# Four-layer image network on one core, scan layer: y kept in the order of the scan in two buffers, its copy-out in two halves, empty turns around the DMAs of the normalizations

## The chip, the core and the metric

The kernel runs on one core of a Trainium2 chip. The metric is the device time of one execution in microseconds. The kernel before takes 12470.36 us (median of 3 runs, 12468.33 to 12488.72).

The engines go by short names: PE multiplies matrices, ACT applies functions and copies, DVE and POOL work element by element, SP issues the DMAs. Each executes its own list of instructions in the order in which the program emits them; what one needs of another it waits for. A wait therefore holds up everything behind it on its engine.

## The reference, cut to what matters

Four layers follow one another on a tensor of 8 images x 64 channels x 64 x 64. Only the first, the scan layer, is touched. For each image it normalizes over the channels, projects to 128 channels (and a gate z), convolves 3x3 to get u, and then runs a recurrence over the 4096 pixels in four directions k: 0 along rows, 1 along columns, 2 and 3 the same two backwards.

```python
def step(h, inp):
    u_t, dt_t, B_t, C_t = inp
    h = h * jnp.exp(dt_t[..., None] * A) + dt_t[..., None] * B_t[:, :, None, :] * u_t[..., None]
    return (h, jnp.einsum('bkcn,bkn->bkc', h, C_t))
...
y = out_y[:, 0] + inv[:, 0] + wh + invwh
...
y = _ln(y, outnorm_g, outnorm_b, LN_EPS) * jax.nn.silu(z)
return jnp.einsum('bhwd,cd->bhwc', y, outproj_w) + outproj_b
```

h has 16 states n for each of the 128 channels. y is the sum over the 16 states and over the four directions, put back into the order of rows; it is normalized over the channels (the output norm), multiplied by the gate and projected back.

## The kernel before

**Tiling.** The 128 channels lie on the partitions. An image has 16 steps s: four directions, each in four chunks of 1024 pixels. The directions follow one another in the order 0, 2, 1, 3 (the last image: 1, 3, 0, 2), so steps 0 to 7 go along rows and 8 to 15 along columns. A step has 16 units, one for each state n, and the program is written as one long list of *turns*, one turn for a unit (the loop at L919). The whole list is laid down by hand (manual_schedule), so the order on each engine is the order of emission.

**A unit (L757).** ACT makes a = exp(dt x A) (L719). z = B x dt x u comes in one of two ways. For the 12 states outside BY_POOL, PE spreads B over the partitions into PSUM (L737) and DVE multiplies it (L764). For states 0, 3, 6 and 8, POOL multiplies a broadcast B loaded by DMA (L727) and ACT copies it to PSUM (L734). DVE scans (L768), POOL multiplies by the broadcast C (ct, L773), and PE adds the product into the PSUM tile yps (L810). The broadcast tiles of C come by a DMA of 512 KB each on SP's queue (L715), into five buffers; a load has to wait until PE has read the buffer's former content.

**The sum of a step.** There is a single yps tile. Products trail the units by three turns. In turn 3 of a step, the last step's sum has just been completed in turn 2, so `empty` (L779) has ACT copy it into y (L783), and `begin_sum` (L790) starts the next sum by a matmul that adds what y holds already: the identity (or, for the last sums, the centring matrix lno_cen) times y, or in the first direction skipd times u (L801). Turn 7 does two sum_ups to catch up. At two steps of an image (3 to 4 and 11 to 12), where a direction turns round on the same chunk, yps is simply kept: no copy and no begin. So an image has 14 copies and 14 begins. y lies in the order of rows, in one of two buffers that alternate by image. In the column steps (k odd), `ordered` (L588) makes a view with a step of 64 elements, and both the copy (write) and the begin (read) go through it.

**The background queue (L166 to L231).** All other work of the layer is cut into small items (a make, mostly one matmul on PE, and a use one turn later, on ACT or DVE): the projections of the next step (`lower`, `step_size`), the whole preparation of the next image (loads of x, input norm `norm_x`, projections, gates, convolution in five pieces a block), and the output norm of the image before (`norm_y`, `after`). One item is taken per turn (`bg.before`, L926 and L931). In the turns named `idle` (3, 6, 7, 8; L898) only an item without a make may be taken. `none` is an item that does nothing: an empty turn. Items of the next step go ahead of the others; pieces of the convolution alternate with the queue.

**A normalization** computes variances on PE, and ACT puts each as a row and SP sends it to DRAM (`put`, L335). Then a chain (L358) follows: `fetch` reads all variances back over 128 partitions (DMA, L345), `root` (ACT, L348), `invert` (DVE, L351, then a DMA to DRAM, L352), `back` (DMA, L356). Then `apply` has PE spread the result (L393, L445), DVE multiply by it (L398, L450) and ACT add gain and bias; for the output norm POOL multiplies by the gate (L566) and PE projects (L572, L573). The output norm of image b-1 is queued in step 0 of image b; its blocks of x and of z are loaded by two DMAs per block (L559, L561), the first three blocks at once, just before `back` (L459). The last image's own output norm goes two blocks at a time in steps 13 to 15, with two items taken per turn, and the last two blocks follow after the last unit.

Of the kernel before, what the change touches and what calls it, by code (L numbers as in the profile page):

```python
# [165 lines left out]
class Background:  # L166
# [7 lines left out]
    def __init__(self):  # L174
        self.queue, self.last, self.late = deque(), None, []
        self.groups, self.open, self.done = deque(), deque(), {}
        self.first = self.credit = 0
        self.item = False

# [42 lines left out]
    def finish(self, b, count):  # L222

        while self.done.get(b, NBK) < count:
            self.credit = 1
            self.before(slots=NBK)
            self.after()

# [6 lines left out]
def scan_layer(cm, x_in, w, xh):  # L235

    tc, nc = cm.tc, cm.nc
    with ExitStack() as ctx:
# [90 lines left out]
        def inverse_root(nb):  # L329
# [27 lines left out]

            chain = [none, (None, fetch), none, (None, root), (None, invert), none, (None, back), none]  # L358
            return put, chain, sm

        def norm_x(xn, pairs, project_in):

# [47 lines left out]
            for i in pairs:  # L410
                out += [project_in(2 * i), project_in(2 * i + 1)]
                if i + 2 in pairs:
                    out.insert(-1, apply(i + 2))
            return out

        def norm_y(y, blocks, load, multiply, project_out):
# [40 lines left out]
            out = [(None, lambda _: [square(j) for j in blocks[:2]]), none]  # L457
            out += [variance(j) for j in blocks] + chain
            out.insert(-2, (None, lambda _: [load(j) for j in blocks[:3]]))  # L459
            out += [apply(j) for j in blocks[:2]]  # L460
# [3 lines left out]
            for j in blocks:  # L464
                if j + 2 in blocks:
                    out.append(apply(j + 2))
                    if j + 2 == blocks[-1]:
                        out.append(end)
                out.append(project_out(j))
            return out  # L470
# [4 lines left out]
        def before(b):  # L475
# [72 lines left out]
            for pairs in FIRST if b == 0 else (range(NBK // 2),):  # L548
                items.append(norm_x(xn, pairs, project_in))
            return u, zd, items, [gate(j) for j in range(NBK)], [convolve(j) for j in range(NBK)]  # L550
# [226 lines left out]
        full = []  # L777

        def empty():  # L779

            if full:
                ctl = full.pop()
                nc.scalar.copy(  # L783
                    ordered(ctl["y"], ctl["k"], ctl["c"]),
                    ctl["ps"].rearrange("p (a b) -> p a b", b=S),
                )

        kept = []

        def begin_sum():  # L790


            ctl = pending[0][0]
            if kept:
                ctl["ps"] = kept.pop()
                return
            ctl["ps"] = psy.tile([DI, CH], F32, name="yps", tag="yps")
            wt, src = (skipd, ctl["u"]) if ctl["new_y"] else (ctl["mat"], ctl["y"])
            so, half = ordered(src, ctl["k"], ctl["c"]), BK // S
            for i in range(CH // BK):  # L800
                nc.tensor.matmul(  # L801
                    ctl["ps"][:, bass.ts(i, BK)].rearrange("p (a b) -> p a b", b=S),
                    wt, so[:, i * half : (i + 1) * half, :], start=True, stop=False,
                )
# [26 lines left out]
        def prepare(b, s):  # L831

            if b not in images:
                return None
            u, zd, y = images[b]
# [8 lines left out]
            ctl = dict(  # L844
                k=k, c=c, u=u, y=y, dt=dt, bc=low["bc"][k // 2], ut=ut, dus=e, soft=soft, new=new, state=None,
                first=(i == 0), new_y=(s < NCH), turns=(s % (2 * NCH) == NCH - 1),
# [9 lines left out]
        def start(b):  # L856
            u, zd, items, gates, convs = before(b)
            y = io.tile([DI, L], F32, name="y", tag="y")
            images[b] = (u, zd, y)
            bg.add(items[0] + items[1])  # L860
# [11 lines left out]
        with tc.manual_schedule():  # L872
# [15 lines left out]
            for b in range(NB):  # L888
                for s in range(4 * NCH):
# [29 lines left out]
                    for n in range(N):  # L919
# [30 lines left out]
                        if s == 0 and n == LAG + 2 and b > 0:  # L950
                            bg.add(after(b - 1, images[b - 1][2], images.pop(b - 1)[1]))
                        if late and n == LAG + 2:
                            c = 4 * NCH - s
                            bg.add(after(b, images[b][2], images[b][1], range(2 * c, 2 * c + 2)))
                        if s == (1 if b else NCH) and n == 0 and b + 1 < NB:
# [9 lines left out]
            empty()  # L965
            bg.add(after(NB - 1, images[NB - 1][2], images[NB - 1][1], range(2)))
            bg.drain()
# [1148 lines left out]
```

## Time and profile before

One execution was profiled. Its parts (windows of the trace; the scan layer's units run from the first to the last L768):

| what | us |
|---|---|
| time of the profiled execution | 12474.25 |
| its span | 12472.4 |
| before the first unit | 93.48 |
| units of the scan layer, 8 images x 16 steps | 7074.05 |
| of it: POOL busy | 6680.89 |
| of it: DVE busy | 6564.59 |
| of it: PE busy | 6497.71 |
| of it: ACT busy | 4898.81 |
| all behind the last unit (rest of the layer, the other three layers) | 5304.9 |
| image 0 / image 1 / image 3 / image 7 | 939.39 / 869.32 / 870.31 / 913.96 |

The profile's page gives busy time by engine, then the span in slices, the DMA queues, the chain of work that ended last, and groups of instructions by line. In a group's row, the count stands behind the x, then the busy time in us and the mean of one in ns, and behind the bar the idle time of the engine just before these instructions with what ended it. A window's row gives start and end, length, then the busy time of PE, weight loads, DVE, ACT and POOL (with counts), the clock granted to PE (1.00 is full), the busy share of the DMA engines and GB/s. One float32 matmul of 512 columns stands in the trace as two PE records.

### The profile page before, as it was taken

The page shows a single profiled execution, that of the slowest core. Times are in us where ns is not written, and L with a number is a line of the kernel's source. Part 1 is how long each engine was busy: PE and PEld are TensorE (multiplying, and loading weights), DVE is VectorE, ACT ScalarE, POOL GpSimd, SP SyncE. Part 2 cuts the span into 40 slices and gives each one's busy share as a digit, 9 for nine tenths or more (in the row PEclk, how much of TensorE's full clock was granted, in tenths as well). Part 3 has the DMA queues.
Part 4 walks back from the last instruction along what each step waited for, and adds up shares of the span by engine and source line. Part 5 has one row for each costly group of instructions (what it writes and reads, how often), then busy time and mean ns, then how long its engine had stood idle before and what let it go on. Part 6 is the DMA issues. An engine that isn't in the chain of part 4 may idle for free. (4 is left out here: it accounts for less than half of the span.)

```text
span 12472.4 us, 119759 instructions
## 1 busy us (share of the span) xinstructions
PE 11350.5 (91%) x38827; PEld 4100.1 (33%) x38827; DVE 10374.0 (83%) x7334; ACT 7820.0 (63%) x10296; POOL 7404.9 (59%) x3510
## 2 busy tenths in 40 slices
PE   7899998999999999999998889999987778999999
PEld 2233332332333323323322232332334463333333
DVE  4999999999999999999989857768687785676767
ACT  4776766766766767767666545546456584555554
POOL 4999999999999999999999800000005490000000
PEclk8999999999999999999989889999998789999999
DMA  3666656656666666666566510000011100000000
GB/s 110 208 210 211 210 200 221 211 202 214 210 203 212 207 212 213 202 218 205 198 206 204 179 34 18 12 25 6 18 38 40 41 24 23 17 6 17 6 11 6
DMA packets 541331, 1562.17 MB, mean 125 GB/s; under 512 B 127360, under 2 KB 144400, under 8 KB 538128
## 3 DMA queue, kind: packets, MB, share of 16 engines
q1 hardware_dynamic: 540688, 1554.36, 37.8%
q8 instruction: 310, 5.08, 0.2%
q14 instruction: 333, 2.73, 0.1%
HBM read 1456.41 MB, written 88.87 MB: 124 GB/s over the span
## 5 line engine op out<-in xcount | busy, mean ns | idle before, releaser
L773 POOL TENSOR_TENSOR ct<-ct,h 128x1024 f32<-128x1024 f32 x2048 | 4796.5, 2363 | 391.5 <-DMA ct<-bc 183.9
L768 DVE TENSOR_TENSOR_SCAN h<-a,state,z 128x1024 f32<-128x1024 f32 x1536 | 3572.4, 2342 | 96.0 <-ACT z L734 43.0
L1117 DVE TENSOR_TENSOR sum<-sum,ex 128x1024 f32<-128x1024 f32 x1920 | 2347.5, 1223 | 617.9 <-ACT ex L1110 483.0
L1110 ACT ACTIVATE ex<-sc 128x1024 f32<-128x1024 f32 x2048 | 1968.0, 1024 | 1359.7 <-PE sc L1105 1359.3
L810 PE MATMUL yps<-ct,ident 128*128 128x512 f32 x5632 | 2810.5, 629 | 6.9 <-POOL ct L773 6.8
L719 ACT ACTIVATE a<-dt,amat 128x1024 f32<-128x1024 f32 x2048 | 2345.0, 1146 | 718.1 <-DVE h L768 711.7
L764 DVE TENSOR_TENSOR z<-z,e 128x1024 f32<-128x1024 f32 x1536 | 1865.9, 1215 | 310.9 <-PE z L737 196.0
L1124 PE MATMUL av<-ex,v 128*64 128x512 f32 x8192 | 1950.0, 604 | 0.0
L1105 PE MATMUL sc<-q,k 16*128 16x512 f32 (+1 forms) x8192 | 1562.2, 623 | 4.2 <-ACT q L1098 3.1
L810 PEld LDWEIGHTS yps<-ct,ident 128*128 128x128 f32 x5632 | 1009.0, 194 | 1390.9 <-issue 1253.2
L737 PE MATMUL z<-bs,pick 48*128 48x512 bf16 x3072 | 957.0, 393 | 447.0 <-DVE h L768 398.5
L810 PE MATMUL yps<-ct,lno_cen 128*128 128x512 f32 x2560 | 1313.1, 646 | 0.5 <-POOL ct L773 0.5
L768 DVE TENSOR_TENSOR_SCAN h<-a,z 128x1024 f32<-128x1024 f32 x512 | 1163.1, 2283 | 80.8 <-ACT z L734 51.2
L727 POOL TENSOR_TENSOR bt<-bt,e 128x1024 f32<-128x1024 f32 x512 | 1210.8, 2365 | 4.5 <-DMA bt<-bc 4.5
L1431 POOL TENSOR_TENSOR gt<-gt,pad 128x1024 f32<-128x1024 f32 x16 | 34.9, 2184 | 1571.1 <-ACT gt L1430 1492.5
L1124 PEld LDWEIGHTS av<-ex,v 128*64 128x64 f32 x8192 | 512.2, 136 | 1332.8 <-issue 1278.9
L734 ACT COPY z<-bt 128x1024 f32<-128x1024 f32 x512 | 519.7, 1015 | 589.0 <-POOL bt L727 316.4
L1105 PEld LDWEIGHTS sc<-q,k 16*128 16x128 f32 (+1 forms) x8192 | 528.4, 184 | 1016.1 <-issue 977.2
L737 PEld LDWEIGHTS <-pick 48*128 48x128 bf16 x3072 | 177.7, 95 | 1709.6 <-DVE h L768 888.0
L810 PEld LDWEIGHTS yps<-ct,lno_cen 128*128 128x128 f32 x2560 | 468.6, 198 | 637.3 <-issue 560.7
L530 PE MATMUL vps<-pad,convd 128*128 128x512 f32 x1152 | 545.9, 597 | 0.0
L1804 DVE RECIPROCAL r<-e 128x512 f32<-128x512 f32 x128 | 420.6, 3322 | 0.0
(416 smaller groups left out, 10539.4 us busy)
## 6 DMA issues: line engine op xcount, KB each, us to landing
ct<-bc SPq DMA_DIRECT2D x2048, 512.0 KB
bt<-bc SPq DMA_DIRECT2D x512, 512.0 KB
x<-x SPq DMA_DIRECT2D x12, 2048.0 KB
bc<-e SPq DMA_DIRECT2D x128, 128.0 KB
zd<-z SPq DMA_DIRECT2D x64, 256.0 KB
z<-zd SPq DMA_DIRECT2D x64, 256.0 KB
x<-x SPq DMA_DIRECT2D x32, 512.0 KB
part<-x SPq DMA_DIRECT2D x128, 128.0 KB
```

The source lines that it names most:

```text
L530: nc.tensor.matmul(held[0].rearrange("p (r c) -> p r c", c=S), convd[:, t, :], pad[:, j * rows + dy : (j + 1) * rows + dy, dx : dx + S], s ...
L719: ctl["exp", n] = nc.scalar.activation(ctl["a", n], ctl["dt"], AF.Exp, scale=amat[:, ctl["k"], n : n + 1])
L727: nc.gpsimd.tensor_tensor(bt, bt, ctl["dus"], ALU.mult)
L737: nc.tensor.matmul(z[:, bass.ts(i, BK)], pick[:, n : n + 1].to_broadcast([3 * N, DI]), ctl["bs"][:, bass.ts(i, BK)], start=True, stop=True,)
L764: first = nc.vector.tensor_tensor(z, z, ctl["dus"], ALU.mult)
L768: nc.vector.tensor_tensor_scan(h[:, flip], a[:, flip], z[:, flip], 0.0 if state is None else state[:, n : n + 1], ALU.mult, ALU.add,)
L773: freed[at] = nc.gpsimd.tensor_tensor(ct, ct, h, ALU.mult)
L810: nc.tensor.matmul(ctl["ps"][:, bass.ts(i, BK)], ctl["mat"], ct[:, bass.ts(i, BK)], start=False, stop=(n == N - 1 and not ctl["turns"]),)
L1105: nc.tensor.matmul(sc[:, e, :], k[r : r + d, bass.ts(j, 128)], qs[i][r : r + d, :], start=True, stop=True,)
L1110: nc.scalar.activation(ex, sc, AF.Exp)
L1117: nc.vector.tensor_tensor(sums[i], sums[i], ex, ALU.add)
L1124: nc.tensor.matmul(avs[i][r, :], v[:, j, r], ex[:, e, :], start=(j == 0), stop=(j == TQ - 1))
```

## The change

1. **y in the order of its direction.** An image has up to two y tiles, "row" and "col", made when first written. `into` says which layout a step's sum is written to: the one that the next reader reads. A begin always reads its own layout, without a step (`own`). Where the next direction is of the other kind, the copy writes with a step of 64 instead. The sums of steps 4 to 7 are so written with a step (into "col"), and those of 12 to 15 (into "row"); steps 0 to 2 and 8 to 10 write and read without one. In the last image, only steps 4 to 7 write with a step, and the begins of steps 0 to 3 read u with one, as before.
2. **Two buffers.** Each layout has its own tag with one buffer, which alternate by image. The second layout of image b takes the buffer that holds the result of image b-1, so before it is first written (turn 3 of step 5) `flush` empties the queue up to the mark that ends b-1's output norm.
3. **The copy in halves**: two copies of 512 instead of one of 1024.
4. **Chains**: 11 items instead of 8, with two empty turns between fetch and root and three behind back (one each before).
5. **norm_y**: the loads of the first three blocks lie between the variances, and an empty turn follows each project_out. **norm_x** (images after the first): an empty turn behind each pair.
6. **Turn 3 is no longer idle**: an item with a make may be taken there; its matmul stands before the begin.

```diff
+    def flush(self, b):
+        while b >= 0 and b not in self.flushed:
+            self.before()
+            self.after()
...
-            chain = [none, (None, fetch), none, (None, root), (None, invert), none, (None, back), none]
+            chain = [none, (None, fetch), none, none, (None, root), (None, invert), none]
+            chain += [(None, back), none, none, none]
...
-            out += [variance(j) for j in blocks] + chain
-            out.insert(-2, (None, lambda _: [load(j) for j in blocks[:3]]))
+            for j in blocks:
+                out.append(variance(j))
+                if j in blocks[1:6:2] or nb == 2:
+                    at = j if nb == 2 else j0 + (j - j0) // 2
+                    out.append((None, lambda _, at=at: load(at)))
+            out += chain
...
-                out.append(project_out(j))
+                out += [project_out(j), none]
...
+        def layout(b, name):
+            im = images[b]
+            if name not in im:
+                first = ("row", "col")[steps(b)[0][0] % 2]
+                if name != first:
+                    bg.flush(b - 1)
+                at = b % 2 if name == first else 1 - b % 2
+                im[name] = io.tile([DI, L], F32, name="y", tag=f"y{at}", bufs=1)
+            return im[name]
+        def own(t, c):
+            return t[:, bass.ts(c, CH)].rearrange("p (a b) -> p a b", b=S)
...
-                nc.scalar.copy(
-                    ordered(ctl["y"], ctl["k"], ctl["c"]),
-                    ctl["ps"].rearrange("p (a b) -> p a b", b=S),
-                )
+                mine = ("row", "col")[ctl["k"] % 2]
+                dst = layout(ctl["b"], ctl["into"])
+                out = own(dst, ctl["c"]) if ctl["into"] == mine else ordered(dst, 1, ctl["c"])
+                half = BK // S
+                for i in range(CH // BK):
+                    nc.scalar.copy(
+                        out[:, i * half : (i + 1) * half, :],
+                        ctl["ps"][:, bass.ts(i, BK)].rearrange("p (a b) -> p a b", b=S),
+                    )
...
-            wt, src = (skipd, ctl["u"]) if ctl["new_y"] else (ctl["mat"], ctl["y"])
-            so, half = ordered(src, ctl["k"], ctl["c"]), BK // S
+            if ctl["new_y"]:
+                wt, so = skipd, ordered(ctl["u"], ctl["k"], ctl["c"])
+            else:
+                mine = ("row", "col")[ctl["k"] % 2]
+                wt, so = ctl["mat"], own(layout(ctl["b"], mine), ctl["c"])
...
+            ks = [steps(b)[q * NCH][0] % 2 for q in range(4)] + [0]
+            q = s // NCH
...
+                b=b, k=k, c=c, u=u, into=("row", "col")[ks[q + q % 2]], ...
...
-                    idle = () if early or late else (3, 6, 7, 8)
+                    idle = () if early or late else (6, 7, 8)
...
+                            bg.add([(None, lambda _, b=b - 1: bg.flushed.add(b))])
```

More of the change, by code (lines that the diff above doesn't have):

```diff
@@ L177, in __init__ @@
         self.first = self.credit = 0
+        self.flushed = set()
         self.item = False
@@ L356, in back, with norm_x @@
                 nc.sync.dma_start(sm["r"], rs.rearrange("(j f) -> j f", j=nb))
-            chain = [none, (None, fetch), none, (None, root), (None, invert), none, (None, back), none]
+            chain = [none, (None, fetch), none, none, (None, root), (None, invert), none]
+            chain += [(None, back), none, none, none]
             return put, chain, sm
-        def norm_x(xn, pairs, project_in):
+        def norm_x(b, xn, pairs, project_in):
             put, chain, sm = inverse_root(2 * len(pairs))
@@ L413, in norm_x @@
                     out.insert(-1, apply(i + 2))
+                if b:
+                    out.append(none)
             return out
@@ L548, in before @@
             for pairs in FIRST if b == 0 else (range(NBK // 2),):
-                items.append(norm_x(xn, pairs, project_in))
+                items.append(norm_x(b, xn, pairs, project_in))
             return u, zd, items, [gate(j) for j in range(NBK)], [convolve(j) for j in range(NBK)]
@@ L797, in begin_sum @@
             ctl["ps"] = psy.tile([DI, CH], F32, name="yps", tag="yps")
-            wt, src = (skipd, ctl["u"]) if ctl["new_y"] else (ctl["mat"], ctl["y"])
-            so, half = ordered(src, ctl["k"], ctl["c"]), BK // S
+            half = BK // S
+            if ctl["new_y"]:
[3 more added lines that the diff above has]
+                wt, so = ctl["mat"], own(layout(ctl["b"], mine), ctl["c"])
             for i in range(CH // BK):
@@ L834, in prepare @@
                 return None
-            u, zd, y = images[b]
+            u = images[b]["u"]
             k, c, i = steps(b)[s]
+            ks = [steps(b)[q * NCH][0] % 2 for q in range(4)] + [0]
+            q = s // NCH
             bg.finish(b, 2 * c + 2 if s < NCH and k == 0 else NBK)
@@ L844, in prepare @@
             ctl = dict(
-                k=k, c=c, u=u, y=y, dt=dt, bc=low["bc"][k // 2], ut=ut, dus=e, soft=soft, new=new, state=None,
+                b=b, k=k, c=c, u=u, into=("row", "col")[ks[q + q % 2]], dt=dt, bc=low["bc"][k // 2], ut=ut, dus=e, soft=soft, new=new, state=None,
                 first=(i == 0), new_y=(s < NCH), turns=(s % (2 * NCH) == NCH - 1),
@@ L857, in start @@
             u, zd, items, gates, convs = before(b)
-            y = io.tile([DI, L], F32, name="y", tag="y")
-            images[b] = (u, zd, y)
+            images[b] = {"u": u, "zd": zd}
             bg.add(items[0] + items[1])
@@ L950, in scan_layer @@
                         if s == 0 and n == LAG + 2 and b > 0:
-                            bg.add(after(b - 1, images[b - 1][2], images.pop(b - 1)[1]))
+                            last = images.pop(b - 1)
+                            bg.add(after(b - 1, last["row"], last["zd"]))
+                            bg.add([(None, lambda _, b=b - 1: bg.flushed.add(b))])
                         if late and n == LAG + 2:
                             c = 4 * NCH - s
-                            bg.add(after(b, images[b][2], images[b][1], range(2 * c, 2 * c + 2)))
+                            bg.add(after(b, images[b]["row"], images[b]["zd"], range(2 * c, 2 * c + 2)))
                         if s == (1 if b else NCH) and n == 0 and b + 1 < NB:
@@ L965, in scan_layer @@
             empty()
-            bg.add(after(NB - 1, images[NB - 1][2], images[NB - 1][1], range(2)))
+            last = images[NB - 1]
+            bg.add(after(NB - 1, last["row"], last["zd"], range(2)))
             bg.drain()
```

## Prediction

> **What bounds the kernel now.** Only the scan layer is touched, so I look at its units (7074.05 us of the span). First the groups by line:
>
> ```profile
> L773 POOL TENSOR_TENSOR ct<-ct,h 128x1024 f32<-128x1024 f32 x2048 | 4796.5, 2363 | 391.5 <-DMA ct<-bc 183.9
> ...
> L764 DVE TENSOR_TENSOR z<-z,e 128x1024 f32<-128x1024 f32 x1536 | 1865.9, 1215 | 310.9 <-PE z L737 196.0
> ```
>
> POOL's multiply is the costliest, and half of POOL's idle time ends with a ct load; DVE's idle time ends with PE. POOL is busy 6680.89 of 7074.05 us, so no more than 393 us can be had while its work stays as it is. The change takes none of it away. Then windows by step; the borders are every 16th start of L768 in the timeline. Image 3, steps 1, 2, 7, 9, 11, 14 and the sum:
>
> ```profile
> 2820.81:2872.94 52.13, 43.36 (x103) 14.47 (x102) 51.04 (x30) 38.03 (x58) 52.13 (x25) 1.00 0.68 211
> 2872.94:2933.81 60.87, 56.99 (x123) 17.79 (x124) 54.00 (x34) 37.59 (x57) 55.51 (x28) 0.92 0.69 225
> ...
> 3148.25:3205.51 57.26, 53.38 (x117) 18.95 (x118) 51.31 (x29) 46.37 (x63) 50.45 (x25) 0.91 0.65 205
> ...
> 3366.18:3422.43 56.25, 51.77 (x114) 18.37 (x114) 51.03 (x30) 38.18 (x52) 51.23 (x23) 0.94 0.57 194
> ...
> 3526.85:3582.98 56.13, 51.64 (x114) 18.37 (x114) 51.03 (x29) 35.77 (x49) 51.70 (x23) 0.94 0.57 187
> ...
> sum 870.31, PE 812.05 PEld 274.44 DVE 820.76 ACT 614.48 POOL 836.48; mean PE 50.75 PEld 17.15 DVE 51.30 ACT 38.41 POOL 52.28
> ```
>
> Step 1 is POOL without a gap. The others stand 4 to 6 us above POOL's work: 33.8 us in this image. Why, the timeline of PE in step 14 shows, then two windows before and in it:
>
> ```profile
> 3536.24 0.60 PE L737 MATMUL z<-bs,pick 48*128 48x512 bf16 x2 [0.85 <-DVE h L768]
> 3537.99 3.68 PE L801 MATMUL yps<-y,lno_cen 128*128 128x512 f32 x4 [1.15 <-ACT y L783]
> 3541.61 1.03 PE L737 MATMUL z<-bs,pick 48*128 48x512 bf16 x2
> 3542.57 3.78 PE L810 MATMUL yps<-ct,lno_cen 128*128 128x512 f32 x4
> ```
>
> ```profile
> 3536.20:3539.60 3.40, 2.21 (x4) 0.62 (x5) 3.36 (x3) 3.40 (x5) 3.40 (x3) 1.00 0.60 188
> 3539.60:3543.00 3.40, 3.40 (x6) 0.87 (x5) 2.55 (x2) 2.61 (x5) 3.40 (x2) 0.50 0.00 0
> ```
>
> PE waits for ACT's copy, reads y with a step for 3.68 us, and its clock is halved, so that the first sum takes 3.78 us. Until then no ct buffer is free; SP stands on it, and nothing moves on the DMA engines (0.00). In SP's waits for image 3:
>
> ```profile
> SPq L715 <- PE yps L810: 619.6, 238, 11.5
> ```
>
> The 11.5 us is this wait. The bill comes at units 5 and 7: DVE waits 0.85 and 3.70 us for z, POOL 4.4 us for a sum and two ct loads.
>
> **The change, part by part.** The sum is made against the profiled execution, 12474.25 us (span 12472.4), 3.9 above the median.
>
> *The begin without a step.* L801 by form, in columns and in rows of image 3:
>
> ```profile
> L801 PE MATMUL yps<-y,lno_cen 128*128 128x512 f32 x16 | 14.7, 1052 | 4.1 <-ACT y L783 4.1
> L801 PE MATMUL yps<-u,skipd 128*128 128x512 f32 x16 | 7.9, 618 | 1.2 <-ACT y L783 1.2
> ```
>
> Four records make a begin: 14.7/4 = 3.68 against 7.9/4 = 1.98, so 1.70 us less at 7 begins an image (steps 8, 9, 10, 11, 13, 14, 15). In step 14, unit 7's wait of 3.70 loses 1.70, and half of the clock's loss (a sum of 1.88 at full clock took 3.78; half is 0.95). The matmuls of the item that now goes ahead of the begin (four convolution records, 2.02) fill the 1.15 us gap and push 0.9 behind it, but leave a later turn, where PE is not waited for. So the wait falls by 1.7 to 2.7, POOL's 4.4 by about 2.5. POOL's idle time in steps 9 to 15 is 0.6 + 1.2 + 5.0 + 0 + 3.2 + 4.4 + 4.9 = 19.3 us; I take a little over half, **-10** an image. What is late next is z for unit 7 again, behind the begin, two sums and three items.
>
> *The copies.* L783 in image 3, shortest, median, longest:
>
> ```profile
> L783 ACT COPY y<-yps x14: 1004/1462/1941, 2778.4 to 3593.7; 128x1024 f32<-128x1024 f32 x14
> ```
>
> 1.00 us plain, 1.94 with a step. A half in plain form is like L337 (512 from PSUM): 0.57, so a pair costs 0.14 more. No row shows a half with a step. It lies between 0.57 and the 1.94 of a whole one; I take 1.0, by the whole one's half. An image has 8 copies with a step instead of 7: about 3 us more on ACT, which is idle for 255 us of an image. On the path they move: those read by steps 9 to 11 become 0.8 faster, those in steps 5 to 8 slower by 1.0. Whether a begin may start on the first half alone no row shows: 0 if it waits for both, up to 1.0 better; I take 0, since each begin here follows the end of the copy. In steps 5 and 6 PE waited 0.3 us for the plain copy, so most of the 1.0 is open there where nothing with a matmul stands in turn 3 (step 5: a load of x): +2 an image. Against it stands step 7: PE waited 3.37 us for the copy, behind the gates' table loads on ACT, and lost 3.78 - 1.98 to the clock. By the new count of turns gates come in turns 9 and later of steps 9 to 11, but for one in turn 4: -4. Together **-2**.
>
> The ScalarE page of the Trainium skill (ScalarE: Activation LUTs, What ACT_TABLE_LOAD costs) gives ACT one element a cycle for every function, which knows no step. The 1.94 against 1.00 says otherwise and decides. By the page the copies with a step would cost like plain ones, and the sum would be some 14 us lower.
>
> *The output norm* (steps 2 to 4, images 1 to 6). In step 2 DVE waits 3.6 us for `apply` and PE 6.5 for the last DMA, which went out behind six loads. I counted the turns by the rules of `before`: now back is taken in turn 9 of step 2 and the first apply in turn 13, four turns of 3.3 us, and no load stands before back on SP. POOL's idle 5.4 us in step 2 goes but for one: **-4**. The gates' multiplies (8 x 1.28) move from steps 2 and 3 to 3 and 4; POOL has no gap there, so they cost what they did.
>
> *More turns.* An image gets 21 more items (3 + 3 in the chains, 4 behind pairs, 2 for the loads, 8 behind project_out, the mark), and turn 3 gives 16 places. Before, by the same count, four turns in each of steps 11 to 14 and eight in step 15 took nothing. By the count nothing is forced; the mark is taken in turn 15 of step 4, the flush stands in turn 3 of step 5 and finds it: 0. Were it half a step late, the last three blocks would run without units between: three times a projection of some 1.9 us behind a multiply of 1.3 on POOL and 0.8 on ACT, 12 us an image.
>
> The Trainium skill speaks against empty turns: TensorE: Matmul & The Clock Gate, section Why this matters for your kernels, wants no idle gap of over some 3 us on PE, else a window at half clock. Here half clock followed gaps of 0.85 and 1.15 us, with PE busy for 2.21 of 3.40, so the row is the harsher one. By the rule the clock's share would not be won in steps 11, 13 and 14, and the sum would be 7 x 3 x 0.95 = 20 us smaller.
>
> *Image 0*, steps 0 and 1: root and back are taken up to one turn earlier in the crowded queue, the apply in turn 5 as before; DVE's wait there is 5.9 us: **-5** for both steps. *Image 7*: step 2 lasts 70.36 with 12.2 us of POOL idle, since back came two turns before apply; now four: -11. Its steps 5 to 7 lose their reads with a step: -3. Steps 13 to 15 (70.59, 66.24, 62.79): DVE waits there 13.6 us for apply and 12.9 for root. By the count fetch and root, and back and apply, each come one turn of 3.3 us farther apart: at most 9.9 + 8.8, I take 16. Together **-30**. *Behind the last unit*: back no longer goes out behind four loads of some 0.55 us: **-2**.
>
> Sum: images 0 to 6, 7 x (-10 - 2) = -84; images 1 to 6, 6 x -4 = -24; -5, -30, -2: **-145**. 12474.25 - 145 = 12329, against the median **12325**.
>
> **The rivals.**
> 1. *Half of it comes back.* For: POOL and DVE both stand within 6% of the step, so a gap closed on one opens on the other; the item before the begin can eat what the read saves. Against: step 1 shows that a step can run without a gap. Then -5 an image for begins, 0 for copies, norms two thirds: -35 - 40 = -75, 12395; up to 12445.
> 2. *The gaps go nearly all.* For: the clock no longer drops. Then POOL's idle 393 falls to the 83 of image 0's first three steps and some 60: -250, 12220.
> 3. *Nothing*: z for unit 7 is late for the sums and items ahead of it alone, and the norms' waits turn into others; 12470.
> 4. *Slower, at the copies with a step in steps 5 to 8.* PE then waits there over 2 us and its clock halves, as in step 7 now (57.26, 5.5 above its neighbour of 51.63). 4 steps x 8 images x 5.5 = +176, and of the sum -145 + 28 (step 7) - 14 (the +2, counted here) = -131 stay: +45, 12515. It decides if the gap before L801 there reaches 2 us. Against: turn 3 now has a matmul in steps 7 and 8.
>
> **The numbers.** Forecast (12290 to 12390) 0.56; rival 1 (12390 to 12445) 0.20; rival 2 (below 12290) 0.12; rival 3 0.06; rival 4 0.06. A measurement of this kernel tells about 0.2%, 25 us, from no change. Faster 0.88, same 0.06, slower 0.06. The unknown half with a step, at 1.94, would add 0.94 x 2 x 4 x 7 = 53 us, a begin on the first half take off some 30; both lie within 12240 to 12440, which leaves out some of rivals 1 and 2 and all of 3 and 4.
>
> **What would show it.** L801 at 0.6 us a record but for image 7's u; L783 at 0.57 and about 1.0; SP's longest waits in steps 11 to 15 down from 11.5 to about 8; step 14 near 53, step 2 near 53 and steps 3 and 4 near 57 and 55; step 7 near 53; image 7's last steps near 60. Wrong would be: steps 5 and 8 above 55, clock 0.91 there, or DVE's wait for z at unit 7 unchanged.

## The result and the profile after

The kernel after takes 12327.19 us (median of 4 runs, 12321.73 to 12331.92), against 12469.35 us of the kernel before in runs beside it: a ratio of 0.9883, 95% interval 0.9867 to 0.9898, or 142 us less. Its profiled execution took 12328.75 us (span 12326.7), 145.5 less than that of before. The units of the scan layer make 6924.22 us instead of 7074.05, which is 149.8 less; what lies ahead of them grew by 0.9 and what lies behind by 3.2 (other runs vary there by as much). The figures below leave out one single run, of the kernel a_lay, that took 34485.76 us; no trace shows why. Line numbers are 14 higher or more: L787 is POOL's multiply (L773 before), L778 DVE's (L764), L782 the scan, L817 the copy into y, L839 the begin, L848 the sum, L729 the load of ct.

First the units as one window of the trace, with the columns of the windows before:

```profile
94.40:7018.62 6924.22, 6347.59 (x14492) 2159.45 (x14492) 6549.36 (x3695) 4898.50 (x7013) 6674.46 (x2999) 0.97 0.64 210
```

DVE, ACT and POOL do nearly the same work as before. PE is busy 150 us less: 94 of it in the begins that read y (257.3 us before, 163.7 after), while the mean granted clock rose from 0.96 to 0.97. POOL's free time fell from 393 to 250 us. The groups by line show where that time was:

```profile
L787 POOL TENSOR_TENSOR ct<-ct,h 128x1024 f32<-128x1024 f32 x2048 | 4794.6, 2364 | 248.2 <-DVE h L782 113.3
...
L778 DVE TENSOR_TENSOR z<-z,e 128x1024 f32<-128x1024 f32 x1536 | 1863.3, 1213 | 221.1 <-PE z L751 143.2
```

Of POOL's idle time before its multiply, the part that ends with a ct load fell from 183.9 to 79.0 us. The part that ends with DVE's scan fell less, from 136.0 to 113.3, and is now the largest. The windows of image 3, steps 1, 2, 7, 14 and the sum of all 16:

```profile
2776.70:2831.62 54.92, 48.19 (x113) 14.77 (x112) 50.92 (x29) 40.31 (x62) 53.67 (x25) 1.00 0.67 229
2831.62:2884.87 53.25, 47.74 (x108) 15.47 (x108) 52.23 (x33) 35.27 (x55) 53.25 (x26) 0.97 0.67 215
...
3101.46:3154.85 53.39, 51.19 (x116) 16.68 (x116) 52.96 (x33) 37.77 (x57) 52.68 (x26) 0.97 0.61 207
...
3467.09:3520.24 53.15, 49.27 (x114) 17.77 (x114) 50.88 (x30) 35.80 (x50) 51.45 (x23) 0.97 0.58 196
...
sum 847.74, PE 786.34 PEld 269.03 DVE 818.23 ACT 614.46 POOL 835.48; mean PE 49.15 PEld 16.81 DVE 51.14 ACT 38.40 POOL 52.22
```

Step 2 fell from 60.87 to 53.25, step 7 from 57.26 to 53.39, step 14 from 56.13 to 53.15. Step 1 goes the other way, 52.13 to 54.92; more of that below. The image lost 22.6 us, more than its like: images 1 to 6 lost 13.7 on average.

The timeline of PE at the begin of step 14, the place that the prediction took apart:

```profile
3477.74 1.99 PE L544 MATMUL vps<-pad,convd 128*128 128x512 f32 x4
3479.57 1.88 PE L839 MATMUL yps<-y,lno_cen 128*128 128x512 f32 x4
3481.38 0.60 PE L751 MATMUL z<-bs,pick 48*128 48x512 bf16 x2
3481.91 1.99 PE L848 MATMUL yps<-ct,lno_cen 128*128 128x512 f32 x4
```

No line has an idle time in brackets. The item in turn 3 (a piece of convolution) fills the place where PE waited for the copy, the begin takes 1.88 us instead of 3.68, and the first sum 1.99 instead of 3.78, since the clock stays at 1.00. The copies of image 3 (shortest, median and longest), and SP's waits for a ct buffer there (total, times, longest):

```profile
L817 ACT COPY y<-yps x28: 574/1038/1128, 2786.2 to 3584.0; 128x512 f32<-128x512 f32 x28
```

```profile
SPq L729 <- PE yps L848: 598.5, 236, 10.3
```

Halves take 0.57 plain and 1.04 us with a step, as forecast. The longest of SP's waits, 10.3 us, lies in step 5. In steps 11 to 15, for which about 8 was forecast, the longest is now 7.9 us (11.5 before).

**Where the time went, by steps.** Differences after minus before of the step lengths, in us (images 1 to 6: sum over the six, with the prediction's term beside it):

```
                          predicted   measured
images 1-6, steps 0, 1          0      +24.3
            steps 2 to 4      -24      -43.4
            steps 5 to 8      -12      -28.9
            steps 9 to 15     -60      -34.3
image 0,    steps 0, 1         -5      -11.0
            steps 2 to 15     -12       -7.6
image 7                       -30      -49.0
behind the last unit           -2       +3.2
```

The total is right within 5 us, but five of the terms are off by 17 to 26 us, and they cancel. So the experiments ask what each part is worth, and why the first row has a plus.

### The profile page after: what moved, and what is told of

It reads as the page before. It is cut to its first block, busy times and chain, and to the rows that moved or that the text cites. A ratio compares the mean times of both kernels' runs of the same rounds, so it can differ in the third digit from the quotient of the medians.

```text
span 12326.7 us, 120038 instructions
## 1 busy us (share of the span) xinstructions
PE 11203.1 (91%) x38827; PEld 4075.9 (33%) x38827; DVE 10359.2 (84%) x7334; ACT 7820.8 (63%) x10409; POOL 7399.3 (60%) x3510
## 5 line engine op out<-in xcount | busy, mean ns | idle before, releaser
L787 POOL TENSOR_TENSOR ct<-ct,h 128x1024 f32<-128x1024 f32 x2048 | 4794.6, 2364 | 248.2 <-DVE h L782 113.3
L782 DVE TENSOR_TENSOR_SCAN h<-a,state,z 128x1024 f32<-128x1024 f32 x1536 | 3573.1, 2342 | 118.2 <-ACT z L748 67.1
L848 PE MATMUL yps<-ct,ident 128*128 128x512 f32 x5632 | 2809.0, 630 | 2.5 <-POOL ct L787 2.4
L778 DVE TENSOR_TENSOR z<-z,e 128x1024 f32<-128x1024 f32 x1536 | 1863.3, 1213 | 221.1 <-PE z L751 143.2
L848 PEld LDWEIGHTS yps<-ct,ident 128*128 128x128 f32 x5632 | 1006.4, 194 | 1384.2 <-issue 1220.6
L848 PE MATMUL yps<-ct,lno_cen 128*128 128x512 f32 x2560 | 1276.3, 630 | 0.0
L782 DVE TENSOR_TENSOR_SCAN h<-a,z 128x1024 f32<-128x1024 f32 x512 | 1162.7, 2282 | 81.4 <-ACT z L748 57.2
L848 PEld LDWEIGHTS yps<-ct,lno_cen 128*128 128x128 f32 x2560 | 458.1, 193 | 618.3 <-issue 564.2
L544 PE MATMUL vps<-pad,convd 128*128 128x512 f32 x1152 | 550.9, 602 | 12.9 <-ACT e L648 12.9
```

The lines of the kernel that those rows point to most:

```text
L544: nc.tensor.matmul(held[0].rearrange("p (r c) -> p r c", c=S), convd[:, t, :], pad[:, j * rows + dy : (j + 1) * rows + dy, dx : dx + S], s ...
L778: first = nc.vector.tensor_tensor(z, z, ctl["dus"], ALU.mult)
L782: nc.vector.tensor_tensor_scan(h[:, flip], a[:, flip], z[:, flip], 0.0 if state is None else state[:, n : n + 1], ALU.mult, ALU.add,)
L787: freed[at] = nc.gpsimd.tensor_tensor(ct, ct, h, ALU.mult)
L848: nc.tensor.matmul(ctl["ps"][:, bass.ts(i, BK)], ctl["mat"], ct[:, bass.ts(i, BK)], start=False, stop=(n == N - 1 and not ctl["turns"]),)
```

## Experiments: one part undone, one part alone

The parts are L (layouts in two buffers with the flush), H (the halves), T (turn 3 open) and C (chains, loads and empty turns). Four kernels undo one part of the kernel after, three add one to the kernel before.

**u_lay: after, without L.** y stays in rows; the copy and the begin of a column step go with a step.

```diff
-                at = b % 2 if name == first else 1 - b % 2
-                im[name] = io.tile([DI, L], F32, name="y", tag=f"y{at}", bufs=1)
+                im[name] = io.tile([DI, L], F32, name="y", tag=f"y{b % 2}", bufs=1)
...
-                out = own(dst, ctl["c"]) if ctl["into"] == mine else ordered(dst, 1, ctl["c"])
+                out = ordered(layout(ctl["b"], "row"), ctl["k"], ctl["c"])
...
-                wt, so = ctl["mat"], own(layout(ctl["b"], mine), ctl["c"])
+                wt, so = ctl["mat"], ordered(layout(ctl["b"], "row"), ctl["k"], ctl["c"])
```

> The kernel after, with y back in one layout (rows): reads and writes of the column steps have their step of 64 again, copies in halves, turn 3 and the chains stay changed. Theory (the begin that reads without a step is the largest single part): the four records of a begin go from about 0.6 to 1.03 us in 7 begins an image, steps 8 to 11 and 13 to 15 lose about 9 us an image together, steps 5 to 8 win back 1 to 2 from their plain copies; time 12380 to 12400. Rival (the gain of those steps came from the matmul that now fills turn 3): within 20 us of 12327.

Measured: 12447.3 us, ratio 0.9981 (0.9969 to 0.9992). Without the layouts nearly all is gone, 120 of the 142 us, which is more than either expectation had. In the profiles the units are 112.8 us longer; in images 1 to 6 it is 13.0 an image in steps 9 to 15 and 3.1 in steps 5 to 8. Step 14 of image 3 as a window:

```profile
3518.86:3576.79 57.93, 54.06 (x114) 18.78 (x114) 51.13 (x29) 35.97 (x50) 50.99 (x23) 0.91 0.54 183
```

The step is back at 57.93, although the items in turn 3 have closed the gaps ahead of the begins (PE waits 18.8 us there in all the layer, 61.5 before). The step's mean clock of 0.91 suggests that the clock halved behind the begin, but it did not. PE at the begin and the sum behind it, then a window there:

```profile
3534.41 3.59 PE L832 MATMUL yps<-y,lno_cen 128*128 128x512 f32 x4
...
3538.47 1.98 PE L841 MATMUL yps<-ct,lno_cen 128*128 128x512 f32 x4
```

```profile
3535.90:3539.30 3.40, 3.40 (x7) 0.80 (x6) 1.21 (x2) 2.81 (x5) 2.59 (x2) 1.00 0.00 0
```

The clock is full here. It was half at the start of the step, from 3518.6 to 3528.9 us, after PE had waited 2.78 us for a scan. The begin still takes 3.59 us (1.88 in after), nothing moves on the DMA engines meanwhile (0.00), and behind it DVE waits 2.19 and 1.82 us for z and POOL 3.02 and 2.00 us for loads. So the read with a step costs by its length alone, without a gap before it and without a halved clock behind it. (The other 2.3 us of DVE's waits in this step lie in and just behind the stretch at half clock.)

**u_turn: after, without T** (idle turns 3, 6, 7, 8 again).

```diff
-                    idle = () if early or late else (6, 7, 8)
+                    idle = () if early or late else (3, 6, 7, 8)
```

> The kernel after, with turn 3 idle again as before. Theory: by the count of turns the queue now reaches step 5 too late in every image from 1 to 7, and 5 to 8 items are forced at once in its turn 3 (the price estimated in the prediction was 12 us an image, 84 in all); together with 1 to 2 us an image for begins that wait uncovered, 12400 to 12430, with step 5 near 60 us. Rival (forced items are hidden beside POOL's work, and the filled turn is worth nothing): 12320 to 12350, step 5 below 55.

Measured: 12357.29 us, 0.9903 (0.9885 to 0.992): 30 us slower than after, between the two expectations. By a count of the turns, 8 items have to be taken in one turn at the flush (turn 3 of step 5) in images 2 to 6, and 5 or 6 in images 1 and 7. Steps 4 and 5 of image 3 (the flush is in the second):

```profile
2934.59:2993.65 59.06, 56.53 (x113) 17.50 (x112) 51.81 (x33) 35.27 (x52) 53.82 (x26) 0.86 0.64 209
2993.65:3055.60 61.95, 54.13 (x120) 17.28 (x120) 51.60 (x31) 38.18 (x58) 55.48 (x26) 0.94 0.63 199
```

In after they last 54.50 and 53.27. The mean over images 1 to 6 is +8.3 in step 5 and +3.1 in step 4, near the 12 us that the prediction gave as the price of a late flush; 4.6 come back in step 1 (a_row below shows why). Steps 6 and 7, whose copies have no matmul beside them here, are not longer (-2.1 and -0.4).

**u_chain: after, without C.**

```diff
-            chain = [none, (None, fetch), none, none, (None, root), (None, invert), none]
-            chain += [(None, back), none, none, none]
+            chain = [none, (None, fetch), none, (None, root), (None, invert), none, (None, back), none]
...
-                if b:
-                    out.append(none)
...
-            for j in blocks:
-                out.append(variance(j))
-                if j in blocks[1:6:2] or nb == 2:
-                    at = j if nb == 2 else j0 + (j - j0) // 2
-                    out.append((None, lambda _, at=at: load(at)))
-            out += chain
+            out += [variance(j) for j in blocks] + chain
+            out.insert(-2, (None, lambda _: [load(j) for j in blocks[:3]]))
...
-                out += [project_out(j), none]
+                out.append(project_out(j))
```

> The kernel after, with the chains, the loads of the output norm and the empty turns as before; layouts, halves and turn 3 stay changed. Theory: step 2 of images 1 to 6 goes back up by about 7 us, image 7 by 12 in step 2 and by 28 in steps 13 to 15, image 0 by about 8 in steps 0 and 1: about 90 in all, 12405 to 12425. Rival (the empty turns give back elsewhere what they save, as step 1 with 4.8 us more hints): 12320 to 12360.

Measured: 12375.01 us, 0.9919 (0.9902 to 0.9935), 48 us slower; the units of its profile, taken in the fastest of the four runs (12358.38), are 33.4 us longer than after's. That is less than expected, because the chains also take something: without them steps 0 and 1 of images 1 to 6 are 3.9 us an image shorter and steps 9 to 15 4.5 us. What they bring lies in image 0 (10.8 in steps 0 and 1), image 7 (15.3 in steps 13 to 15) and steps 2 to 8 (9.7 an image). In images 1 to 6 as a whole C is worth no more than 7.5 us.

The trace shows what C moves. PE's records of the convolution in image 3, in steps 5 to 8 and in steps 9 to 15, in before (L530); behind the length stand PE's busy time with these records, their count, then clock, DMA share and GB/s:

```profile
3042.76:3258.12 215.36, 16.04 (x34) 0.97 0.62 207
3258.12:3638.49 380.37, 52.72 (x111) 0.96 0.60 203
```

The same in after (L544):

```profile
2993.99:3204.94 210.95, 0.00 (x0) 0.97 0.65 212
3204.94:3572.64 367.70, 60.22 (x126) 0.99 0.65 213
```

The other 18 records of after come in step 0 of the next image. Images 1 to 6 have on average 33.7 records in steps 5 to 8, 110.3 in steps 9 to 15 and none in steps 0 and 1 before; after has 0, 129.0 and 18.0, and u_chain 36.0, 108.0 and 0. So the longer list carries convolution out of steps 5 to 8 into steps 9 to 15. The steps that lose records are the shorter ones (u_chain is 6.7 us an image longer in steps 5 to 8), and those that get more are the longer ones (4.5).

**u_half: after, without H.**

```diff
-                half = BK // S
-                for i in range(CH // BK):
-                    nc.scalar.copy(
-                        out[:, i * half : (i + 1) * half, :],
-                        ctl["ps"][:, bass.ts(i, BK)].rearrange("p (a b) -> p a b", b=S),
-                    )
+                nc.scalar.copy(out, ctl["ps"].rearrange("p (a b) -> p a b", b=S))
```

> The kernel after, with one copy of 1024 instead of two halves. Theory (a begin waits for the end of both halves, so halves gain only that the first half can start before the sum's second half is done): within 15 us of 12327, 12320 to 12345. Rival (the begin's first matmul starts on the first half alone): each of 112 begins starts 0.5 to 1.0 us later without halves, 12370 or more.

Measured: 12332.31 us, 0.9883 (0.9862 to 0.9905), the time of after. The halves are worth nothing that can be measured. The trace of after shows the wait: of its 111 begins that follow a copy, none starts before the second half's copy has ended (the smallest gap is 0.05 us). That holds for the 31 that read u as for the 80 that read y. What all share with the copy is the tile yps, which the copy reads and the begin overwrites; no run gave it a second buffer.

**a_lay: before, with L alone.** This is after with the edits of u_turn, u_chain and u_half together.

> The kernel before with the layouts and two buffers alone (one copy of 1024, turn 3 idle, old chains and loads). Theory (the layouts alone carry most of the gain, by the PE time of the begins and the clock behind them; with the rest in place they were worth 16 us an image): steps 9 to 15 fall by 10 to 13 us an image, steps 5 to 7 rise by up to 4 since nothing covers their copies with a step; 12355 to 12395. Rival (the layouts pay only when turn 3 covers the copy; without it the steps 5 to 8 take back what the begins save): 12430 to 12470.

Measured: 12365.94 us (median of three runs, 12353.91 to 12386.67), 0.9913 (0.9894 to 0.9933). L alone brings 88.6 us between the profiles; its profiled run was the slowest of the three. Steps 9 to 15 gain 11.8 us an image (the prediction said 10), and step 14 is 52.1 to 52.3 us in each of images 0 to 6. But steps 5 to 8 lose 3.0 an image: steps 5 to 7, whose begins read what was copied with a step, lose 4.3, and step 8 gains 1.3. The begins of the whole layer, x the count of records, with the idle time of PE just before them:

```profile
L827 PE MATMUL yps<-y,ident 128*128 128x512 f32 x192 | 109.6, 699 | 52.9 <-ACT y L808 52.7
L827 PE MATMUL yps<-y,lno_cen 128*128 128x512 f32 x128 | 67.7, 654 | 24.5 <-ACT y L808 24.3
```

The same two groups in the kernel after:

```profile
L839 PE MATMUL yps<-y,ident 128*128 128x512 f32 x192 | 101.0, 652 | 20.0 <-ACT y L817 20.0
L839 PE MATMUL yps<-y,lno_cen 128*128 128x512 f32 x128 | 62.7, 614 | 3.4 <-ACT y L817 3.4
```

PE waits 77 us for copies with L alone (before: 35.5 + 26.0 = 61.5) and 23 in after, where turn 3 gives it a matmul to do meanwhile.

**a_turn: before, with T alone** (`idle` is (6, 7, 8)).

> The kernel before with turn 3 no longer idle, nothing else. Theory (the item in turn 3 fills PE's wait for the copy but stands before a begin that still reads with a step; and the queue is not late in this kernel, so there is nothing forced to avoid): -30 to +15, 12440 to 12485. Rival (filling turn 3 is itself worth the 27 us that the kernel after lost without it): 12430 to 12450 with step 5 unchanged and steps 8 to 15 lower by 3 or more an image.

Measured: 12474.1 us, 1.001 (1.0001 to 1.002). Alone, the open turn is worth nothing, although PE's wait for the copies ahead of the begins fell from 61.5 to 8.5 us. Filling that wait buys nothing by itself; a likely reason is that the matmul that fills it also moves the begin back, which still reads with a step. The nothing is a sum: step 2 of images 1 to 6 gains 4.6 us an image and step 2 of image 7 10.3, steps 5 to 8 lose 3.4 an image, steps 9 to 15 1.8, and image 0 loses 17.3.

**a_chain: before, with C alone** (the edit of u_chain the other way round).

> The kernel before with the new chains, the spread loads and the empty turns alone. Theory (image 7's last steps gain some 15 to 28, its step 2 some 4 to 12, image 0 about 11; in images 1 to 6 step 2 gains 4 to 8, but the variances and blocks that come later take most of it back): -30 to -60, 12410 to 12440. Rival (the longer queue, with four idle turns a step, pushes convolution pieces and output blocks into steps that had none): 12455 or more.

Measured: 12450.32 us, 0.9986 (0.9977 to 0.9996), 10 us above the range expected and below the rival's. Image 7 gains 42.8 us, 29.8 of it in its last three steps; image 0 3.9; images 1 to 6 *lose* 20.5. Steps 9 to 15 are 8.7 an image longer there, most of it in steps 12 and 15. The 20 items more of C push the convolution back, so that 18 of its records now lie in step 15 (none before) and 39 in steps 0 to 2 of the next image. The first of image 7's last three steps:

```profile
6969.94:7027.05 57.11, 50.93 (x108) 16.11 (x108) 52.41 (x33) 37.24 (x54) 53.46 (x24) 0.91 0.63 201
```

This step lasted 70.59 us before the change and lasts 58.86 in after. So in image 7's last steps C alone gives all of what after gained there (29.8 against 28.1), without help from the layouts.

The three parts alone sum to -88.6 + 10.2 - 26.3 = -105 us in the profiles, together with H they make -150. The parts need each other. What is shown is that C's longer list needs T, or else it reaches L's flush too late (u_turn; in a_lay, with the short list and turn 3 idle, the count gives no item at the flush). That T also covers the copies that L makes slow is inferred: steps 5 to 7 lose 4.3 us in a_lay, while in after the step in the copies costs nothing (x_plain); but in u_turn, without T, steps 6 and 7 lose nothing either.

## Experiments: the copies with a step, and the plus in steps 0 and 1

**x_plain: after, every copy without a step.**

```diff
-                out = own(dst, ctl["c"]) if ctl["into"] == mine else ordered(dst, 1, ctl["c"])
+                out = own(dst, ctl["c"])
```

> The kernel after, where every copy writes plainly, so that the sums of steps 4 to 7 and 12 to 15 land in the wrong order of pixels; it leaves out the reordering of y, and its output is not the reference's. Theory (the prediction's price: a copy with a step is some 0.9 us longer, and in steps 5 to 8 about half of that is open): 2 to 3 us an image in steps 5 to 8 and as much in 13 to 15, 25 to 45 us less than the kernel after. Rival (the item in turn 3 covers the copies): within 12 us of it.

Measured: 12331.77 us, 0.989 (0.9869 to 0.991), beside 12330.21 of after on the same chip. Its copies, shortest, median and longest:

```profile
L817 ACT COPY y<-yps x224: 572/586/616, 183.5 to 7020.8; 128x512 f32<-128x512 f32 x112
```

All 224 take 0.57 to 0.62 us, so the step alone makes the 1.04. ACT is busy 118.6 instead of 170.5 us with them, and those 52 us were worth nothing on the path: the rival's expectation came, and steps 5 to 8 changed by less than 0.1 us an image.

**a_row: after, with its own three buffers for the row of a variance.** ACT waits with the copy of a variance's row (L344) until the DMA before it has read the single buffer: 98.0 us between 1000 and 6200 us of after. It takes T and C together: the same wait is 30.6 us in before, 33.4 in a_turn and 15.9 in a_chain, and undoing either part of after brings it down, to 13.3 in u_turn and 31.5 in u_chain. In step 1 of image 4, ACT's timeline (with the idle time before a line in brackets), then SP's:

```profile
3650.76 0.58 ACT L344 COPY vrow<-vps 1x512 f32<-1x512 f32 x1 [5.42 <-DMA vard<-vrow]
```

```profile
3641.28 6.58 SPq L729 DMA_DIRECT2D ct<-bc  x3
3647.96 0.24 SPq L345 DMA_DIRECT2D vard<-vrow  x1
```

The row's small DMA stands on SP behind loads of ct, and those wait 6.58 us for free buffers. Meanwhile ACT stands, and behind it the copies of z, for which DVE waits 7.6 us in this step.

```diff
-                t = work.tile([NBK, BK], F32, name="vrow", tag="rstd", bufs=1)
+                t = work.tile([2, BK], F32, name="vrow", tag="vrow", bufs=3)
```

> The kernel after, with three buffers of their own for the rows of variances that ACT puts (before: one buffer, shared with the result of back). Theory (step 1 is 4.8 us longer than before, because ACT waits up to 7.3 us for the DMA of the first row, which stands behind a ct load on SP, and unit 8's copy to PSUM stands behind ACT): ACT's 98 us of waits for vard go, step 1 of images 1 to 6 falls by 3 to 5 us: -20 to -30 to after, 12297 to 12310. Rival (step 1 is longer since POOL and PE there hold more work): step 1 unchanged, 12320 to 12335.

Measured: 12303.09 us (12295.37 to 12329.59), 0.9875 (0.9858 to 0.9891). Step 1 of images 1 to 6 is 4.4 us an image shorter, about the +4.1 of steps 0 and 1. As its slowest run was as slow as after, the next runs held after itself as a control.

**after_again: the control.**

> The kernel after once more, on the chip of the runs beside it, as their measure: 12320 to 12335. Both theories of the other runs expect the same of it.

Measured: 12330.21 us (12328.05 to 12333.88), 0.9888 (0.9869 to 0.9908).

**a_own: after, with an own tile for the rows of `lower`.** In after, ACT waits 85.7 us (6.7 before) to write e, until a DMA has read rows that `lower` keeps in the same tile.

```diff
-                    nc.scalar.copy(e[: 4 * N, bass.ts(i, BK)], ps[: 4 * N])
+                    if i == 0:
+                        low["lo"] = work.tile([4 * N, CH], F32, name="lo", tag="lo", bufs=1)
+                    lo = low["lo"]
+                    nc.scalar.copy(lo[:, bass.ts(i, BK)], ps[: 4 * N])
...
-                        e[: 4 * N, bass.ts(i, BK)],
+                        lo[:, bass.ts(i, BK)],
```

> The kernel after, where the rows that lower makes have a tile of their own instead of lying in e. Theory (with turn 3 open, step_size comes a turn earlier and ACT's write to e waits up to 2.9 us for the DMA that still reads the rows from it, 85.7 us in all; but ACT has slack and DVE waits only some 4 us for it): the wait for bc goes, time 0 to 12 us less than the kernel after beside it. Rival (ACT's wait holds PE and the copies behind it and is a main cost of turn 3): 25 us less or more.

Measured: 12326.88 us (12313.41 to 12336.06), 0.9882 (0.9861 to 0.9903). The wait is gone (no idle time at all stands before that write) and the time is the same: nobody waited for ACT there.

**a_both: a_own, and two buffers for the tag of the row.**

```diff
-                t = work.tile([NBK, BK], F32, name="vrow", tag="rstd", bufs=1)
+                t = work.tile([NBK, BK], F32, name="vrow", tag="rstd", bufs=2)
...
-                sm["r"] = work.tile([NBK, BK], F32, name="rstd", tag="rstd", bufs=1)[:nb]
+                sm["r"] = work.tile([NBK, BK], F32, name="rstd", tag="rstd", bufs=2)[:nb]
```

> The kernel after, with the tile of a_own and two buffers shared by the rows of variances and the result of back. Theory: the 20 to 24 us that three own buffers gave in step 1 come as well with two, and what a_own gives adds to it: 20 to 35 us less than the kernel after beside it, 12290 to 12310. Rival (two buffers are too few, since the third row meets the first's DMA again): within 12 us of a_own.

Measured: 12306.54 us (12291.18 to 12313.81), 0.987 (0.985 to 0.989): 24 us below the control on the same chip, and no run of the one reaches into the runs of the other. Against a_own, from which it differs by the second buffer alone, it is 20 us. ACT's copies of the row in after, then in a_both:

```profile
L344 ACT COPY vrow<-vps 1x512 f32<-1x512 f32 x64 | 36.7, 573 | 91.4 <-DMA vard<-vrow 76.1 <-PE vps L438 15.2
```

```profile
L344 ACT COPY vrow<-vps 1x512 f32<-1x512 f32 x64 | 36.5, 571 | 15.9 <-PE vps L438 15.6
```

The wait for the DMA is gone. Step 1 of image 4, first after, then a_both:

```profile
3624.90:3684.16 59.26, 54.83 (x123) 16.36 (x121) 51.03 (x29) 39.87 (x62) 56.12 (x26) 0.94 0.66 216
```

```profile
3619.80:3671.53 51.73, 48.87 (x115) 14.79 (x113) 50.88 (x29) 40.76 (x63) 51.73 (x25) 1.00 0.74 244
```

POOL works without a gap again, as in before. The images' steps 0 and 1 account for 19 of the 30 us between the profiles (3.2 x 6), and image 7's steps 0 to 4 for 9.8. With the row's wait mended, a_both and a_row are the fastest kernels of this study.

## Why the prediction was right, and where it was not

- **The begin without a step** (-10 an image in steps 9 to 15): the mechanism of the read holds (0.6 us a record, step 14 at 53.15, DVE's wait of 3.70 down to 1.82, POOL's 4.4 to 1.7). The clock's share of it, half of 0.95 us at three begins an image, is not confirmed: of the 36 begins in steps 9 to 15 of images 1 to 6, 14 had a reduced clock in the first sum behind them before, and one has it in a_turn and in u_lay, which keep the read with a step; yet a_turn is no faster than before (the item ahead also moves its begins back), and u_lay only by 25 us. The term's size is 11.8 with the layouts alone. In after it is 5.7, and what failed is the step "More turns ... 0": C costs steps 9 to 15 8.7 us an image on the kernel before and 4.5 in after. By the count of turns nothing is forced, which is right, but the items ahead of them move the convolution to later steps, as u_chain's counts show. Image 6 shows it most: its steps 10 and 11 last 59.2 and 63.7 us (53.6 and 57.8 before). The term came from image 3, which gained 12.7 there; the six range from -12.7 to +4.7.
- **The copies** (-2): a half with a step takes 1.04 us and a begin waits for both halves, as chosen. The "+2 an image" failed: with turn 3 filled it is 0 (x_plain), and with L alone it is 4.3 in steps 5 to 7 (a_lay). Step 7 gained 2.6 on average, of the 4 forecast. What steps 5 to 8 gained beyond the forecast came with C, which took the convolution out of steps 7 and 8 (u_chain: 3.2 and 3.7 us longer).
- **The output norm** (-4 an image): -7.2. Its direction is right, step 2 alone gained 7.8 against the 4 forecast; steps 3 and 4 together moved by 0.6. The chains are not its only cause: C alone gives 4.8 in step 2, and T alone 4.6.
- **Steps 0 and 1** (0): +4.1 an image. This step failed by what was left out. The empty turns and the open turn were costed as places in a queue alone. Together they also brought loads of ct on SP ahead of the row's DMA, and thereby ACT's wait for the row's only buffer. a_row and a_both show that the wait is the cause: with more buffers the plus goes. u_turn and u_chain show that it takes both edits: without either, step 1 is 4.6 or 4.5 us shorter.
- **The flush** (0, or 12 if late): 0 in after, where steps 5 last 1.0 us less than before. When it is late (u_turn), 8.3 + 3.1 us.
- **Image 0** (-5 in steps 0 and 1): -11.0, of which the chains alone give 8.3. Its later steps gained 7.6 of 12.
- **Image 7** (-30): -49.0. The term for steps 13 to 15 was 16 and is 28.1. DVE's three waits there in before, then what of them is left in after (us in total, times, longest):

```profile
DVE y L450 <- PE rps L445: 13.6, 4, 5.4
DVE vsm L351 <- ACT vsm L348: 12.9, 3, 5.5
...
DVE h L768 <- ACT z L734: 8.9, 4, 3.8
```

```profile
DVE h L782 <- ACT z L748: 1.8, 3, 1.1
...
DVE y L460 <- PE rps L455: 0.8, 1, 0.8
```

  The prediction took the first two, and of them no more than one turn of 3.3 us for each; they vanish but for 0.8. The third it left out. ACT stood 16.0 us behind project_out's sum (up to 6.1 at once) and kept copies of z waiting behind it. In after that is 3.8. The empty turn behind each project_out is the likely reason, but no run has it alone.
- **Rival 1** (half of it comes back) describes in part what happened in images 1 to 6: the largest share of POOL's idle time now ends with DVE. But image 7, and steps 2 to 8, gave more than it allowed. **Rival 2** is far off: 250 us of POOL's idle time are left. **Rival 3** falls with the result. **Rival 4** falls with the gap before the begins: 23 us in all the layer, and image 3's step 5 at 53.27, step 8 at 50.09.
- **Two readings of lines.** The prediction puts the gapped steps 4 to 6 us above POOL's work; step 7 stood 6.8 above it. And it names step 9 among the windows that it shows, where they are those of steps 1, 2, 7, 11 and 14.
- **The two rules of the skill.** The copy with a step costs 1.04 against 0.57 us, which the page's one element a cycle (ScalarE: Activation LUTs, What ACT_TABLE_LOAD costs) does not have; the measurement decides, though on the path it made no difference. The rule on idle gaps (TensorE: Matmul & The Clock Gate, Why this matters for your kernels) would have made the prediction's sum 20 us smaller; the mean granted clock of the units rose from 0.96 to 0.97, and step 14 of image 3 from 0.94 to 0.97. Nor do the falls of the clock follow gaps of that length: of the 62 falls to half between 1000 and 6200 us of before, 59 had no gap of 3 us on PE in the 3.4 us ahead of them.

So the total was right by luck in part, because errors cancelled: 60 us were forecast that did not come (steps 9 to 15 and 0 and 1 of images 1 to 6, image 0's later steps, the tail), and 61 came that were not forecast (steps 2 to 8, image 7, image 0's first steps). Some of the two have one cause, the convolution that left steps 7 and 8 and came to steps 9 to 15. What stays open is how much of the 4.5 us there each moved piece costs, and why T and C only together bring the loads ahead of the row; no run moved the pieces alone.

## What to carry to other kernels

An empty turn in a list laid down by hand is not free: it shifts everything behind it. So count, step by step, which work moves where, and look for who is behind it on each queue, above all for a small DMA that gets behind big loads while its tile has one buffer. A part that is worth nothing alone (the open turn) can be what makes another pay, so undo parts from the end state as well as adding them to the start. A mean clock below 1 in a step does not say that the clock is what the step pays for: look where in the step it was half. And a term read from one image should be checked against two or three others before it is multiplied.

## What the runs showed of the hardware

- A matmul of 512 float32 columns that reads y with a step of 64 elements takes 1.05 us a record on average in image 3, against 0.59 without (begins of 3.68 and 1.88 us). With a step a record is as long at half clock as at full: of the lno_cen begins in the column steps of images 0 to 6 of before, 62 records at full clock have a mean of 1.07 us and 32 at half clock 1.03. Without a step the clock doubles it, 0.59 to 0.62 us at full and 1.06 to 1.10 at half clock. Most of the change's gain comes from the shorter read (u_lay, a_lay).
- ACT's copy of 512 elements a partition from PSUM takes 0.57 us, and 1.04 when it writes with a step of 64 elements: the step of the output alone nearly doubles it (x_plain).
- In step 14 of image 3 of before the clock was half for 6.8 us from 3539.6 us on, behind 3.4 us in which PE was busy for 2.21, with gaps of 0.85 and 1.15 us. With the gaps closed and the read still stepped (u_lay) the clock stayed full at the same begin.
